# The L3 stage of a fused Perceiver kernel, written as one pipeline over tiles of four batches with a fixed TensorE order

## The chip, the cores and the metric

The kernel runs on one core of a Trainium2 chip. The metric is the device time of one execution in microseconds (us); of the kernel before there are three timed runs, and one more execution was taken by the hardware profiler. The engines are TensorE (PE; its weight loads are PEld), VectorE (DVE), ScalarE (ACT), GpSimd (POOL) and SyncE (SP, which issues most DMAs). Each engine takes the instructions of its own queue in order; between engines they wait on semaphores.

## The reference, cut to what matters

Four layers act on x of shape (128 batches, 32 tokens, 128 channels). Each layer has a cross part (xattn), an attention part (attn) and a feed-forward part (ffn). The change touches layer 3 alone:

- xattn: `x = x + rmsnorm(layernorm(x)) @ W_in + b_in + depool`, where the depooled context (Dg, 128x512 per group) was computed long before and lies in DRAM;
- attn: layernorm, one projection to q, k, v, then for each batch and each of 16 heads a 32x32 softmax attention with a relative position bias, the output projection, and `x = x + result + b_out`;
- ffn: layernorm, `relu(xn @ sign(W1) + b1) @ sign(W2) + b2`, added to x. W1 and W2 are reduced to -1, 0, 1 once, ahead of the loop.

All of it is float32. No token of one batch meets a token of another, so the 128 batches can be worked on in any grouping.

## The kernel before, in words

The 4096 rows of x are held in on-chip memory as eight **groups** X[0] to X[7] (128 partitions x 4 x 128; 16 batches each). A group has four **tiles** of four batches (128 rows). `L3` (L1783) runs nine rounds. Round `it` interleaves two generators with `abreast`, 12 pieces of the first against 6 of the second: the first is `xattn13` of group `it` followed by `L3_attn` of group `it`, the second is `L3_ffn` of group `it - 1`. A `yield` ends a piece.

**xattn13** (L1150) loads Dg by a DMA (L1153), takes two sets of statistics (DVE bn_stats and bn_aggr at L200 and L201, `ve` at L216, the power on POOL at L218, twice, with `v` and `s` on DVE at L206, L207, L210 between), normalises on DVE (`xn`, L224), transposes on PE (`pxt`, L231), copies on ACT (`xT`, L1159), multiplies (`ph`, L1163), prepares Dg on POOL (L1164, L1165), adds it to X on POOL (L1166) and adds `ph` to X on DVE (L237).

**L3_attn** (L1810) first does the group's front: statistics, `nb` on DVE (L1801), `xn` on ACT (L1804, four instructions), X plus `bo` on POOL (L1816), transposes (`pxt`, L231), `xT` on ACT (L1820), then `pq` (L1824) with `QT` (L1825), `pk` (L1828) with four masked copies `KM` (L1830), and `pv` (L1835) with `V` (L1836). Then, for each of its four tiles: scores `S` in four blocks of four matmuls (L1844), each block followed by the bias add `E` on DVE (L1845); the row maximum `m` on DVE (L1847); the subtraction on POOL (`E`, L1848); the exponential on ACT (L1849); `Vb`, the values spread into blocks, on POOL (L690); a yield; the 32x32 transposes `ET` on DVE (L1854); sixteen matmuls into `po` (L1859); reciprocal `nm` (L1861) and product `O` (L1863) on DVE; four transposes into `pot` (L1866), copied by ACT to `OT` (L1868); the projection `pw` (L1871), added to X on DVE (L1872); a yield.

**L3_ffn** (L1894) is: statistics, `nb`, `xn` on ACT, X plus `b2` on POOL (L1898), `pxt`, `xT` on ACT (L1902), four matmuls `ph` of 512 columns (L1907) with a relu on ACT each (`hT`, L1908), sixteen matmuls `po` (L1914), the addition to X (L237), and the DMA of the finished group to DRAM (L1918).

What sets the order: nothing in L3 is ordered by hand in the kernel before. A scheduler walks the traced instructions and puts them into the five queues by their dependences, their place in the trace and its own idea of their cost. `queue` (L482), which the kernel already uses in other stages, adds a dependence without a semaphore between successive instructions of one engine, so that their order in the queue is the traced order. On PE that is a fixed order; DVE, ACT and POOL stay with the scheduler.

Buffers around the change: `ht` holds two of each tile buffer (E, Vb, ET, O, OT, m, nm, and QT, KM, V of a group); `hs` and `hf` hold one of each; the PSUM pools hold two banks each: `hpm` (tag m: pxt, ph, pq, pk, pv), `hps` (tag s: the score blocks), `hpo` (tag o: po, pot, pw), `hpf` (tag f: the ffn).

Of the kernel before, what the change touches and what calls it, by code (L numbers as in the profile page):

```python
# [9 lines left out]
FP = mybir.dt.float32  # L10
I32 = mybir.dt.int32
U32 = mybir.dt.uint32
AF = mybir.ActivationFunctionType
ALU = mybir.AluOpType
AX = mybir.AxisListType
# [3 lines left out]
B, T, C = 128, 32, 128  # L19
NG = 8  # L20
NT = 32
H = 16
HD = 8
# [134 lines left out]
def abreast(gens):  # L158

    done = [0] * len(gens)  # L160
    live = set(range(len(gens)))
    while live:
        k = min(live, key=lambda k: (done[k] + 1) / gens[k][0])
        done[k] += 1
        if next(gens[k][1], None) is None:
            live.discard(k)


class Kern:
# [202 lines left out]
    def L0_xattn(self, W):  # L372
        nc = self.nc
        with self.pool("xw") as xw:
# [62 lines left out]
            with self.pool("xc") as xc, self.pool("xs", 2) as xs, \  # L437
# [5 lines left out]
                for n in range(B + 2):  # L443
                    g, i, b = n // 16, n // 4 % 4, n % 4
                    for m in (range(3) if n == 0 else (n + 2,)):
                        if m < B:
                            self.L0_xattn_load(tiles.setdefault(m // 4, {"cT": {}, "cN": {}, "E": {}, "T": {}, "QP": []}), m, xc)
                    t = tiles[n // 4] if n < B else None
# [82 lines left out]
    def L0_xattn_scores(self, st, t, b, js, xs, pss):  # L531

        nc, nsn = self.nc, t["nsn"]
        if js[0] == 0:
            if b == 0:
                t["TL"] = xs.tile([128, 2, 4, 4], FP, tag="TL", name="TL")
            t["E"][b] = xs.tile([128, 4, LK + 1], FP, tag="E", name="E", bufs=3)
            t["nm"] = xs.tile([128, 4], FP, tag="nm", name="nm")
            t["sm"] = xs.tile([128, 4], FP, tag="sm", name="sm")
        E, nm, sm = t["E"][b], t["nm"], t["sm"]  # L540
        for j in js:
            S = pss.tile([128, LK], FP, tag="s")
            for cb in range(2):
                self.follow(st, nc.tensor.matmul(S, lhsT=t["QP"][j][:, cb, b, :, :], rhs=t["cT"][b][:, cb, :], start=cb == 0, stop=cb == 1))  # L544
            m = nm[:, j:j + 1]
            nc.vector.tensor_reduce(m, S, AX.X, ALU.max, negate=True)  # L546
            nc.vector.tensor_tensor(m, m, nsn[:, b, j:j + 1], ALU.min)  # L547
            nc.scalar.activation(E[:, j, 0:LK], S, AF.Exp, bias=m, accum_out=sm[:, j:j + 1])  # L548
        if js[1] == 3:
            d = xs.tile([128, 4], FP, tag="d")  # L550
            nc.vector.tensor_tensor(d, nm, nsn[:, b, :], ALU.subtract)
            nc.scalar.activation(E[:, :, LK], d, AF.Exp)
            nc.vector.tensor_tensor(sm, sm, E[:, :, LK], ALU.add)
            nc.vector.reciprocal(sm, sm)  # L554
# [222 lines left out]
    def dispatch(self, pool, psum, tag, I8, n, k, E, NB):  # L777
# [10 lines left out]
        nc.vector.tensor_reduce(M[:, :, 1:n + 1], OH.rearrange("p i j e -> p e i j"), AX.X, ALU.add)  # L788
        S = pool.tile([128, E, n + 1], FP, tag="dS")
        on = pool.tile([128, E, n + 1], FP, tag="don")  # L790
# [5 lines left out]
        f = lambda x: x.rearrange("p e i -> p (e i)")  # L796
        nc.vector.tensor_tensor_scan(f(S), f(on), f(N1), 0.0, ALU.mult, ALU.add)
        yield 1
# [559 lines left out]
    def L2_xattn_tile(self, g, i, xT, KT, w, yc, ypq):  # L1358
# [15 lines left out]
        sm = yc.tile([128, 4, 4], FP, tag="sm")  # L1374
        return {"cT": cT, "cN": cN, "sm": sm, "E": {}, "ET": {}}

    def L2_xattn_scores(self, st, t, b, q, js, yc, yx, yps):
        nc = self.nc
        N = LK + T
        if q is not None:  # L1380
# [3 lines left out]
            t["E"][b] = yx.tile([128, 4, N], FP, tag="E", name="E")  # L1384
            t["ET"][b] = []
        nm, E, sm = t["nm"], t["E"][b], t["sm"]
# [394 lines left out]


    def L3(self, W):  # L1783
        nc = self.nc
        with self.pool("hq") as hq, self.pool("hs") as hs, self.pool("ht", 2) as ht, self.pool("hf") as hf, \
                self.pool("hpm", 2, PSUM) as hpm, self.pool("hps", 2, PSUM) as hps, self.pool("hpo", 2, PSUM) as hpo, \
                self.pool("hpf", 2, PSUM) as hpf:
            q = self.L3_ffn_signs(W["L3_ffn"], hq, hpf)
            for it in range(NG + 1):
                gens = []  # L1790
                if it < NG:
                    gens.append((12, chain(self.xattn13(it, W["L3_xattn"], hs, hpm), self.L3_attn(it, W["L3_attn"], hs, ht, hpm, hps, hpo))))
                if it:
                    gens.append((6, self.L3_ffn(it - 1, W["L3_ffn"], q, hf, hpf)))
                abreast(gens)

    def normed_act(self, pool, src, mv, rs, tag):

# [8 lines left out]

    def L3_attn(self, g, w, ls, lt, lpm, lps, lpo):  # L1810
        nc = self.nc
        rel = w["rel"].rearrange("p (h k) -> p h k", h=H)
        wo4 = w["wo"].rearrange("p (j c) -> p j c", j=4)
        mv, rs = self.stats(ls, self.X[g], 4, 1e-5)
        xn = self.normed_act(ls, self.X[g], mv, rs, "xn3")
        nc.gpsimd.tensor_tensor(self.X[g], self.X[g], w["bo"].unsqueeze(1).to_broadcast([128, 4, 128]), ALU.add)  # L1816
        ps = lpm.tile([128, 512], FP, tag="m", name="pxt")
        self.transposed(ps, xn)
        xT = ls.tile([128, 512], FP, tag="xT3")
        nc.scalar.copy(xT, ps)  # L1820
        yield 1
        QT = lt.tile([128, 16, T], FP, tag="QT")
        ps = lpm.tile([128, 16, T], FP, tag="m", name="pq")
        nc.tensor.matmul(ps, lhsT=w["wqkv"][:, 0:128], rhs=xT, start=True, stop=True)  # L1824
        nc.scalar.activation(QT, ps, AF.Copy, scale=HD ** -0.5)  # L1825
        KM = lt.tile([128, 4, 16, T], FP, tag="KM")
        ps = lpm.tile([128, 16, T], FP, tag="m", name="pk")
        nc.tensor.matmul(ps, lhsT=w["wqkv"][:, 128:256], rhs=xT, start=True, stop=True)  # L1828
        for k in range(4):
            nc.scalar.activation(KM[:, k], ps, AF.Copy, scale=self.hq[:, k:k + 1])  # L1830
        V = lt.tile([128, 4, H, HD + 1], FP, tag="V")
        nc.gpsimd.memset(V[:, :, :, HD:HD + 1], 1.0)
        ps = lpm.tile([128, 4, H, HD], FP, tag="m", name="pv")
        for i in range(4):
            nc.tensor.matmul(ps[:, i], lhsT=xT[:, i * 128:(i + 1) * 128], rhs=w["wqkv"][:, 256:384], start=True, stop=True)  # L1835
        nc.scalar.copy(V[:, :, :, 0:HD], ps)  # L1836
        yield 1
        for i in range(4):
            E = lt.tile([128, H, T], FP, tag="E")
            for j in range(4):  # L1840
                r = slice(32 * j, 32 * j + 32)
                S = lps.tile([128, 4, T], FP, tag="s")
                for b in range(4):
                    nc.tensor.matmul(S[32 * b:32 * b + 32], lhsT=QT[r, 4 * i + b, :], rhs=KM[r, :, 4 * i + b, :], start=True, stop=True)  # L1844
                nc.vector.tensor_tensor(E[:, 4 * j:4 * j + 4, :], S, rel[:, 4 * j:4 * j + 4, :], ALU.add)  # L1845
            m = lt.tile([128, H], FP, tag="m")
            nc.vector.tensor_reduce(m, E, AX.X, ALU.max)  # L1847
            nc.gpsimd.tensor_tensor(E, E, m.unsqueeze(2).to_broadcast([128, H, T]), ALU.subtract)  # L1848
            nc.scalar.activation(E, E, AF.Exp)  # L1849
            Vb = lt.tile([128, H, 4, HD + 1], FP, tag="Vb")  # L1850
            self.blocked(nc.gpsimd, Vb, V[:, i], HD + 1)
            yield 1
            ET = lt.tile([128, H, T], FP, tag="ET")
            nc.vector.transpose(ET.rearrange("p h t -> p (h t)"), E.rearrange("p h t -> p (h t)"))  # L1854
            ps = lpo.tile([128, 4, 4, HD + 1], FP, tag="o", name="po")
            for k in range(4):
                for j in range(4):
                    h = 4 * j + k
                    nc.tensor.matmul(ps[32 * j:32 * j + 32, k], lhsT=ET[:, h, :], rhs=Vb[:, h], start=True, stop=True)  # L1859
            nm = lt.tile([128, 4, 4], FP, tag="nm")  # L1860
            nc.vector.reciprocal(nm, ps[:, :, :, HD])  # L1861
            O = lt.tile([128, 4, 4, HD], FP, tag="O")
            nc.vector.tensor_tensor(O.rearrange("p b k d -> p k b d"), ps[:, :, :, 0:HD], nm.unsqueeze(3).to_broadcast([128, 4, 4, HD]), ALU.mult)  # L1863
            pt = lpo.tile([32, 4, 4, T], FP, tag="o", name="pot")
            for b in range(4):
                nc.tensor.transpose(pt[:, b].rearrange("p j q -> p (j q)"), O[:, b].rearrange("p k d -> p (k d)"), self.ident)  # L1866
            OT = lt.tile([32, 4, 4, T], FP, tag="OT")
            nc.scalar.copy(OT, pt.rearrange("p b j q -> p j b q"))  # L1868
            pw = lpo.tile([128, 128], FP, tag="o", name="pw")
            for j in range(4):  # L1870
                nc.tensor.matmul(pw, lhsT=OT[:, j].rearrange("p b q -> p (b q)"), rhs=wo4[:, j, :], start=j == 0, stop=j == 3)  # L1871
            nc.vector.tensor_tensor(self.X[g][:, i, :], self.X[g][:, i, :], pw, ALU.add)  # L1872
            yield 1


    def L3_ffn_signs(self, w, qw, qpb):
# [58 lines left out]
```

## Time and profile before

| What | us |
|---|---|
| median of three runs | 5003.25 |
| lowest, highest of them | 4987.8, 5008.44 |
| the profiled execution, its own time | 5049.65 |
| its span, first to last instruction | 5047.9 |
| first statistics of L3's group 0 | at 4688.8 |
| first scores of group 0 (S, L1844) | at 4711.5 |
| starts of `pq` (L1824), groups 0 to 7 | 4705.2, 4739.9, 4784.7, 4826.5, 4875.5, 4915.1, 4955.6, 4992.3 |
| last addition of `pw` to X (L1872) | at 5029.0 |
| last addition of the ffn to X (L237) | at 5044.0 |

Times in the profile are counted from the span's start. A page gives each engine's busy time, the span in 40 slices with the granted TensorE clock (PEclk; 1.00 is full speed), the chain of work that ended last, and the costliest groups of instructions by line; the trace can be asked for the same in any window, for who waited for whom, and for the instructions in order of time. A PE count is of records: one float32 matmul of this kernel is two records, a transpose one.

### The profile page before, as it was taken

The page shows a single profiled execution, that of the slowest core. Times are in us where ns is not written, and L with a number is a line of the kernel's source. Part 1 is how long each engine was busy: PE and PEld are TensorE (multiplying, and loading weights), DVE is VectorE, ACT ScalarE, POOL GpSimd, SP SyncE. Part 2 cuts the span into 40 slices and gives each one's busy share as a digit, 9 for nine tenths or more (in the row PEclk, how much of TensorE's full clock was granted, in tenths as well). Part 3 has the DMA queues.
Part 4 walks back from the last instruction along what each step waited for, and adds up shares of the span by engine and source line. Part 5 has one row for each costly group of instructions (what it writes and reads, how often), then busy time and mean ns, then how long its engine had stood idle before and what let it go on. Part 6 is the DMA issues. An engine that isn't in the chain of part 4 may idle for free. (4 is left out here: it accounts for less than half of the span.)

```text
span 5047.9 us, 90278 instructions
## 1 busy us (share of the span) xinstructions
PE 4255.4 (84%) x33802; PEld 3110.6 (62%) x33802; DVE 3389.1 (67%) x10311; ACT 2350.5 (47%) x6637; POOL 1292.9 (26%) x1309
## 2 busy tenths in 40 slices
PE   7999999999898989875367788988898886879688
PEld 5777676767676766665255565666566653446455
DVE  5336758494948585776645378988898775877444
ACT  4555445454454444422134344545554553763333
POOL 1020211111111102135043522332332323322443
PEclk8999898999999999957588898999999997999677
DMA  4223131314141312245133410010101110000100
GB/s 138 60 59 58 42 63 47 61 42 68 38 73 33 59 49 56 64 99 145 32 99 88 136 44 24 26 33 25 29 28 33 37 42 19 1 1 16 37 12 11
DMA packets 388969, 255.96 MB, mean 51 GB/s; under 512 B 184545, under 2 KB 356961, under 8 KB 388017
## 3 DMA queue, kind: packets, MB, share of 16 engines
q1 hardware_dynamic: 361842, 191.22, 16.2%
q0 software_dynamic: 18240, 58.66, 4.1%
q8 instruction: 267, 4.37, 0.4%
q10 hardware_dynamic: 8448, 0.30, 0.2%
q14 instruction: 172, 1.41, 0.1%
HBM read 211.02 MB, written 39.08 MB: 50 GB/s over the span
## 5 line engine op out<-in xcount | busy, mean ns | idle before, releaser
L218 POOL TENSOR_TENSOR rs<-ve,w_const 128x4 f32<-128x4 f32 (+1 forms) x192 | 190.2, 991 | 1567.4 <-DVE ve L216 1285.8
L544 PE MATMUL S<-cT,q 128*128 128x257 f32 x2048 | 545.2, 406 | 19.3 <-ACT E L548 18.5
L544 PEld LDWEIGHTS S<-cT,q 128*128 128x128 f32 x2048 | 389.7, 200 | 146.9 <-issue 53.9
L546 DVE TENSOR_REDUCE nm<-S 128x1 f32<-128x257 f32 x512 | 214.2, 419 | 337.9 <-PE S L544 336.8
L1389 PE MATMUL S<-cT,QM 128*128 128x289 f32 x1024 | 325.0, 434 | 76.3 <-ACT E L1391 69.7
L548 ACT ACTIVATE E<-S,nm 128x257 f32<-128x257 f32 x512 | 242.7, 475 | 297.5 <-DVE nm L547 296.5
L1391 ACT ACTIVATE E<-S,nm 128x289 f32<-128x289 f32 x512 | 253.7, 500 | 188.8 <-DVE nm L1390 184.7
L724 DVE TENSOR_TENSOR A<-A,elt 128x400 f32<-128x400 f32 (+22 forms) x608 | 290.7, 478 | 4.2
L722 DVE TENSOR_TENSOR elt<-A,row 128x400 f32<-128x400 f32 (+22 forms) x608 | 288.5, 474 | 6.4
L527 PE MATMUL pq<-xT,WQK 128*128 128x128 f32 x2048 | 270.9, 292 | 13.4 <-ACT q L528 13.4
L1389 PEld LDWEIGHTS S<-cT,QM 128*128 128x128 f32 x1024 | 177.0, 197 | 159.0 <-ACT E L1391 69.4
L583 PE MATMUL po<-TA,cN 128*128 128x512 f32 x512 | 270.0, 610 | 4.7 <-DVE xn L224 3.9
L527 PEld LDWEIGHTS pq<-xT,WQK 128*128 128x128 f32 x2048 | 255.5, 202 | 23.7 <-ACT q L528 16.7
L584 PE MATMUL po<-TB,cN 128*128 128x512 f32 x512 | 265.6, 600 | 0.0
L558 ACT ACTIVATE E<-E,sm 128x256 f32<-128x256 f32 x512 | 220.2, 498 | 79.4 <-DVE sm L554 74.5
L241 POOL TENSOR_TENSOR QM<-QT,w_const 128x512 f32<-128x512 f32 x128 | 140.8, 1105 | 438.4 <-PE S L1389 412.9
L1390 DVE TENSOR_REDUCE nm<-S 128x1 f32<-128x289 f32 x512 | 219.9, 449 | 30.0 <-PE S L1389 27.0
L1400 PE MATMUL pt<-w_const,E 128*96 128x128 f32 (+1 forms) x1536 | 235.7, 290 | 0.0
L597 PE MATMUL pout<-WVO,OT 128*128 128x128 f32 x2048 | 234.2, 275 | 0.3 <-ACT OT L585 0.3
L597 PEld LDWEIGHTS pout<-WVO,OT 128*128 128x128 f32 x2048 | 231.7, 192 | 0.9 <-ACT OT L585 0.5
L1400 PEld LDWEIGHTS pt<-w_const,E 128*96 128x96 f32 (+1 forms) x1536 | 182.7, 146 | 61.7 <-issue 37.4
L1721 ACT ACTIVATE E<-S,nm 128x128 f32<-128x128 f32 x512 | 180.3, 399 | 64.5 <-DVE nm L1718 64.5
(526 smaller groups left out, 10351.1 us busy)
## 6 DMA issues: line engine op xcount, KB each, us to landing
cT<-ctxT SPq DMA_DIRECT2D x128, 257.0 KB
cN<-ctx SPq DMA_DIRECT2D x128, 256.0 KB
cT<-ctxT SPq DMA_DIRECT2D x32, 514.0 KB
phik<-PW SPq DMA_DIRECT2D x32, 256.0 KB
phiq<-P SPq DMA_DIRECT2D x32, 256.0 KB
A<-phik SPq DMA_DIRECT2D x128, 64.0 KB
PQ<-phiq SPq DMA_DIRECT2D x32, 256.0 KB
cN<-ctx SPq DMA_DIRECT2D x32, 194.0 KB
```

Source lines behind the costliest of these rows:

```text
L527: self.follow(st, nc.tensor.matmul(ps[:, k, :, :], lhsT=WQK[:, 4 * j + k, cb * 128:(cb + 1) * 128], rhs=t["x"], start=True, stop=True))
L544: self.follow(st, nc.tensor.matmul(S, lhsT=t["QP"][j][:, cb, b, :, :], rhs=t["cT"][b][:, cb, :], start=cb == 0, stop=cb == 1))
L548: nc.scalar.activation(E[:, j, 0:LK], S, AF.Exp, bias=m, accum_out=sm[:, j:j + 1])
L558: nc.scalar.activation(E[:, j, 0:256], E[:, j, 0:256], AF.Copy, scale=sm[:, j:j + 1])
L583: self.follow(st, nc.tensor.matmul(po, lhsT=cN[:, 0, c], rhs=TA, start=True, stop=False), nc.tensor.matmul(po, lhsT=cN[:, 1, c], rhs=TB, s ...
L584: nc.tensor.matmul(po, lhsT=cN[:, 1, c], rhs=TB, start=False, stop=True))
L597: self.follow(st, nc.tensor.matmul(po[:, 0, :], lhsT=OT[:, cb, h, :, :], rhs=WVO[:, cb, h, :], start=h == 0 and cb == 0, stop=False))
L722: nc.vector.tensor_tensor(t, A[:, k, :, i0:i1].rearrange("p h i -> p i h").unsqueeze(3).to_broadcast([128, m, HC, n]), row[:, :, i0:N].uns ...
L724: nc.vector.tensor_tensor(A[:, i0:i1, :, i0:N], A[:, i0:i1, :, i0:N], t, ALU.subtract)
L1389: self.follow(st, nc.tensor.matmul(S, lhsT=t["QM"][:, 0, 4 * j:4 * j + 4, :], rhs=t["cT"][:, b, :], start=True, stop=True))
L1391: nc.scalar.activation(E[:, j, :], S, AF.Exp, bias=nm[:, j:j + 1], accum_out=sm[:, j, b:b + 1])
L1400: self.follow(st, nc.tensor.transpose(pt[0:n, j * 128:(j + 1) * 128], E[:, j, k0:k1], self.ident))
```

## The change

L3 becomes a loop over n = 0 to 33 that works on three tiles at once. `L3_attn` is cut into five parts with the same instructions: `L3_attn_front` (everything up to V), `L3_attn_scores` (S to Vb), `L3_attn_values` (ET, po, nm, O), `L3_attn_turn` (pot, OT) and `L3_attn_end` (pw, the addition to X). Step n traces, in this order: the turn of tile n-2, the scores of tile n, a piece of the next group's prologue, the values of tile n-1, a piece of ffn, the end of tile n-2, a piece of prologue, a piece of ffn. After each, `order` chains the newly traced PE instructions with `queue`, so PE's order is exactly the traced one.

The prologue of group g+1 (xattn13, then the front) is started at the first step of group g; it has four pieces, so it is traced in the first and second step of the group: first step `pxt` and `ph` of xattn, second step `pxt` of the front and `pq`, `pk`, `pv`. The ffn of a group is queued when its last tile has ended, which is in the second step of the next group; its five pieces then come as: `pxt` at the end of that second step, four `ph` in the third step, sixteen `po` in the fourth. No instruction is added or removed, no buffer count is changed.

```diff
     def L3(self, W):
...
-            for it in range(NG + 1):
-                gens = []
-                if it < NG:
-                    gens.append((12, chain(self.xattn13(it, W["L3_xattn"], hs, hpm), self.L3_attn(it, W["L3_attn"], hs, ht, hpm, hps, hpo))))
-                if it:
-                    gens.append((6, self.L3_ffn(it - 1, W["L3_ffn"], q, hf, hpf)))
-                abreast(gens)
+            w = W["L3_attn"]
+            st, traced = {}, nc.cur_bb.bb.instructions
+            at = len(traced)
+            def order():
+                nonlocal at
+                self.queue(st, *[i for i in traced[at:] if i.engine == nc.tensor.engine])
+                at = len(traced)
+            grp = {}
+            def pro(g):
+                return chain(self.xattn13(g, W["L3_xattn"], hs, hpm), self.L3_attn_front(g, w, hs, ht, hpm, grp)) if g < NG else iter(())
+            new, ffn, fq, units = pro(0), iter(()), [], {}
+            for _ in new:
+                order()
+            def side(k):
+                nonlocal ffn
+                if k == 0:
+                    next(new, None)
+                else:
+                    if next(ffn, None) is None and fq:
+                        ffn = self.L3_ffn(fq.pop(0), W["L3_ffn"], q, hf, hpf)
+                        next(ffn, None)
+                order()
+            for n in range(NT + 2):
+                g, i = n // 4, n % 4
+                if i == 0 and n < NT:
+                    for _ in new:
+                        order()
+                    new = pro(g + 1)
+                if n > 1:
+                    pt = self.L3_attn_turn(units[n - 2], ht, hpo)
+                if n < NT:
+                    units[n] = self.L3_attn_scores(grp[g], i, w, ht, hps)
+                order()
+                side(0)
+                if 0 < n <= NT:
+                    self.L3_attn_values(units[n - 1], ht, hpo)
+                order()
+                side(1)
+                if n > 1:
+                    self.L3_attn_end((n - 2) // 4, (n - 2) % 4, units.pop(n - 2), w, hpo)
+                    if n % 4 == 1:
+                        fq.append(n // 4 - 1)
+                order()
+                side(0)
+                side(1)
+            for _ in ffn:
+                order()
+            while fq:
+                for _ in self.L3_ffn(fq.pop(0), W["L3_ffn"], q, hf, hpf):
+                    order()
```

## The prediction

> **What bounds the kernel now.** I read the page first, to see where L3 lies and how TensorE does there.
>
> ```profile
> span 5047.9 us, 90278 instructions
> ...
> PE   7999999999898989875367788988898886879688
> ...
> PEclk8999898999999999957588898999999997999677
> ```
>
> L3 is the last three slices (about 360 us, 7% of the span): PE looks busy, but its granted clock is 0.6 to 0.7 where most other stages have 0.9. Then the busy times of the stage in one window, and who PE and VectorE waited for in it:
>
> ```profile
> core 0: us, PE busy (x) PEld busy (x) DVE busy (x) ACT busy (x) POOL busy (x), PEclk, DMA share, GB/s
> 4690.00:5028.00 338.00, 277.83 (x2961) 177.13 (x2962) 161.01 (x586) 121.29 (x224) 147.89 (x138) 0.72 0.05 14
> ```
>
> ```profile
> PE po L1859 <- DVE ET L1854: 18.6, 13, 5.5
> PE pxt L231 <- ACT xn L1804: 10.5, 6, 5.2
> PE pxt L231 <- DVE xn L224: 8.8, 1, 8.8
> PE po L1859 <- DVE mv L201: 6.5, 4, 1.7
> ```
>
> No engine is full: PE is busy 82% at a clock of 0.72, VectorE and POOL under half. L3 is bound by a chain that runs through all engines, and PE is slow because it pauses. The instructions in order of time show the chain, once per group:
>
> ```profile
> 4906.64 0.69 DVE L237 TENSOR_TENSOR X<-X,ph 128x512 f32<-128x512 f32 x1
> ...
> 4909.83 1.02 POOL L218 TENSOR_TENSOR rs<-ve,w_const 128x4 f32<-128x4 f32 x1 [3.12 <-DVE ve L216]
> ...
> 4911.12 1.64 ACT L1804 ACTIVATE xn<-X,nb,rs 128x128 f32<-128x128 f32 x4
> ...
> 4915.06 2.07 PE L1824 MATMUL pq<-xT,w_L_attn 128*128 128x512 f32 x2 [0.68 <-ACT xT L1820]
> ...
> 4922.35 0.18 PEld L1844 LDWEIGHTS S<-KM,QT 32*32 32x32 f32 x16 [0.76 <-ACT KM L1830]
> ```
>
> From the addition of `ph` to the next group's first scores it is 15.7 us. `pq` starts 40 us apart: 4705.2 to 4992.3 is seven groups in 287.1, **41.0 us per group** (34.7 to 49.0). From first scores (4711.5) to the last addition of `pw` (5029.2) it is 317.7.
>
> **What the change does not alter.** No instruction comes or goes. Queues up to L3 are the same, with the same first group's front, so I keep 4711.5 for the first scores. The last ffn, alone after the last `pw`, stays serial (5029.2 to 5047.9). SP's queue differs in one place: a Dg load now stands ahead of the first output, and no compute waits for an output.
>
> **What it moves.** I read the queues of the changed program as built. In steady state PE does, per group, four steps: A: pot, S, pxt of xattn, po, pw, ph; B: pot, S, pxt of the front, po, pw, pq, pk, pv, pxt of the ffn; C: pot, S, po, two ffn ph, pw, two ph; D: pot, S, po, eight ffn po, pw, eight po. VectorE has the tile's ET ahead of the next tile's score additions, and in A to B: ET, then X plus ph, then the additions of B. POOL has a Vb ahead of the E of A, C and D, and in B: E, rs (front), X plus bo, rs, Vb, rs (both for the next xattn), X plus Dg, rs (ffn), Dg twice, X plus b2. PE can no longer slip other matmuls into a gap, so whatever is late on those queues holds everything behind it.
>
> **The floor, if nothing waited.** PE at full clock, from rows of the timeline (distance to the next instruction): pot and pxt 0.44, po 0.40, pw 1.08, xattn ph 1.1, eight ffn po 1.96, one ffn ph or pq or pk 0.86, pv 1.0; S about 1.4, because its third block waits for the first block's addition (two PSUM banks). Four tiles are 4 x 3.32 = 13.3; the rest is 3 x 0.44 + 1.1 + 1.7 + 1.0 + 3.4 + 3.9 = 12.4. Together 25.7 against 41.0 now. This is what the change could bring at best: 7 x 15.3 = 107 us.
>
> **One steady group, walked through.** Time 0 is the last scores of step A. Durations are the means of the groups by line in L3.
>
> To the front's transposes in B: pxt and po 0.9; Vb (POOL waits for po, because two buffers) 1.18, to 2.1; E 1.05, to 3.15; exponential 0.63, to 3.8; ET 0.71, to 4.55; X plus ph 0.69, to 5.25 (`ph` itself was done at 3.2: it is VectorE's order that holds it). Then VectorE has two additions 0.49, two bn_stats 0.4, two additions 0.5, two bn_aggr 0.25, m 0.69: 7.6; POOL's E 1.05, to 8.7; rs 1.02, to 9.75; nb 0.16; four xn 1.65, to 11.65; transposes done at **11.9**. PE had nothing allowed since B's scores (about 6.3): a gap of over 4 us.
>
> To the ffn's transposes at the end of B, all through POOL: X plus bo 1.27 (it must wait for the four xn), to 12.95; rs 1.0, to 14.0; Vb 1.18, to 15.2; rs 1.0, to 16.25; VectorE: s, four xn, and between them X plus pw, bn_stats, bn_aggr, 1.85, to 18.1; X plus Dg 1.28, to 19.4; rs 1.0, to 20.4; nb 0.2; four xn 1.65, to 22.3; transposes done at **22.55**. Beside this PE does po, pw, pq, pk, pv by about 18, half of it at half clock, which costs nothing there: the cover is 4.5 us. PE pauses again for 2.6 to 4.
>
> PE sets the rest. C: pot, S, po 2.5 (pot cold, 1.03 by its row), to 25.0; two ph at half clock 3.4 (the last ffn took 1.7 each when cold), to 28.4; pw 1.08; two ph 1.75, to 31.2 (E and exponential of C, held to 28.8 by Dg, X plus b2 and Vb on POOL, just do not delay the relus). D: 0.44 + 1.4 + 0.4 + 1.96 + 1.08 + 1.96 = 7.2, to 38.4. A again: 0.44 + 1.4: **40.2**. I counted some 19 hand-overs between engines at about 0.05 us; the timeline shows 0.03 to 0.14, so I add 0.04 each: **41.0 us per group**. The stalls of the four tiles go, but the two layernorm chains, which ran partly beside PE work, now stand in line in step B.
>
> The unknown is the clock after the two gaps, which the trace of before shows only for its own gaps. Lower end: full clock in C, 1.7 less for the two ph and 0.4 for pot, so 38.9 with the hand-overs. Upper end: half clock through C, D and A: pw 0.85 more twice, the other two ph 1.7, sixteen po 3.9, pots 0.85: 8.2 more, 49.2. I take the middle value, half clock until about 28, since the nearest rows show recovery after some 3 to 9 us:
>
> ```profile
> 4888.00:4891.00 3.00, 0.77 (x33) 0.61 (x35) 1.08 (x3) 1.21 (x2) 1.20 (x2) 1.00 0.00 0
> 4891.00:4894.00 3.00, 3.00 (x46) 2.51 (x32) 1.34 (x4) 0.00 (x0) 2.22 (x2) 0.58 0.02 5
> 4894.00:4897.00 3.00, 3.00 (x62) 2.21 (x60) 1.56 (x5) 1.11 (x2) 0.00 (x0) 0.85 0.00 0
> ```
>
> One pause of 2.2 us, and the clock (third number from the end) falls to half and is back some 4 us later. After 4909 it stayed at half until about 4918.4, with PE busy most of that time. The Trainium skill ("TensorE: Matmul & The Clock Gate", Part 1) says that the clock halves after about one idle window of 3.4 us and is full again after one busy window as long; its table at the end asks for no gap above about 3 us, which speaks against a fixed order with a gap of over 4. By that rule alone the second cold stretch costs 1.7 instead of 2.1 per group, 2 us over all groups; the rows here show a shorter pause sufficing and a longer recovery.
>
> **The sum.** First scores to last `pw` addition: first tile 1.4; group 0, which has no ffn and no earlier tiles but the same first chain, 30; six steady groups 6 x 41.0 = 246; the last group and the drain 31.6 (step A 5, the ffn's transposes at 11, C 8.7, D 7.2, to 27; then pot, po and pw of the last two tiles, one after another with nm, O and OT between, 4.6). Together 309 against 317.7: **9 us less**. On the profiled execution that is 5049.65 - 9 = 5040.6; that execution was 46 us over the median of the three runs, and I apply the difference to the median: 5003.25 - 9, **about 4994 us**. Differences under 0.5% (25 us) are about what a measurement of this kernel cannot tell from no change.
>
> **Rivals.** (1) PE-bound steps: the statistics come early enough that B hardly waits. For it: VectorE and POOL are under half busy, and the statistics of the next xattn do move a whole group ahead. Against it: nothing of the front's chain can start before X plus ph. With both chains at half their length beyond PE's own work the group is about 31: 6 x 10 less than forecast, and a little in group 0: 4930. (2) Slower: PE's clock stays at half after the gaps of B, through C, D and A; 49.2 per group, 6 x 8.2 and 6 more in the last group: 5049. It decides from about 5 of those 8.2 us (46 to 47 per group) on. For it: the stage has 0.72 now, and from 4813 to 4828 the clock was at half although PE was busy 2.2 to 3.0 of every 3 us. Against: from 4960 to 4981 it was full with PE as dense as in my C and D. (3) The fixed order costs at every tile: in S, VectorE is busy with ET or a Vb-delayed chain when the third block needs its bank, and nothing may be slipped in; 0.4 us more for 32 tiles is 13 us: 5007.
>
> **Chances and range.** Forecast (38.5 to 43.5 per group, so 15 us either way): 0.66, of which 0.11 lies below the 0.5% bound and 0.02 above it. Rival 1: 0.09, rival 2: 0.17, rival 3: 0.08. Faster 0.11 + 0.09 = 0.20, same 0.53 + 0.08 = 0.61, slower 0.02 + 0.17 = 0.19. Rival 2 comes in degrees, from its point of decision (25 us over the median, 5028) to 5049. The range is the forecast's 15 us with the spread of the runs (about 10) added, and reaches up to 5038, the middle of rival 2: **4965 to 5038**. Outside it lie rival 1, half of rival 2 and some tails, 0.09 + 0.085 + 0.02, just under 2 in 10.
>
> **What would show it.** Right: in step B the front's `pxt` waits for xn on ACT by 4 to 5 us and the ffn's `pxt` by 2 to 5, once per group each; X plus ph starts right behind an ET and not behind `ph`; `pq` starts 39 to 43 us apart; waits of po for ET are gone; the clock falls to half twice per group. Wrong: `pq` under 36 apart (the chains overlap more than the queues say) or over 45 with the clock at 0.5 through the ffn's matmuls; or a wait in S or po that I have at nothing.

## The result, and the profile after

The changed kernel takes 5018.40 us (median of 20 runs, 4999.49 to 5030.58) against 5001.74 of the kernel before in the same session (20 runs, 4987.8 to 5011.76): ratio 1.0032, 95% interval 1.0023 to 1.0041. It is **slower by 16.7 us**; 9 us less had been forecast.

Between two profiled executions the stages ahead of L3, which are the same, differ by tens of us (first scores at 4711.5 before, at 4667.4 after), so I compare L3 from its first scores to its last addition of `pw`, here the one window of that length in the changed kernel (busy us and records of PE, PEld, DVE, ACT, POOL; then the clock):

```profile
4667.40:5000.59 333.19, 256.96 (x2936) 164.07 (x2936) 157.28 (x550) 116.50 (x213) 135.91 (x128) 0.73 0.04 12
```

That is 333.2 us against 317.7 (4711.5 to 5029.3): 15.5 more, close to the 16.7 by which the medians differ. `pq` starts 42.2, 44.8, 44.5, 44.4 and 44.4 us apart from the third on (41.0 on average before). The mean clock is the 0.73 of before. The waits of PE in the stage (us in total, times, longest):

```profile
PE pxt L231 <- ACT xn L1849: 47.8, 14, 4.5
PE S L1891 <- DVE E L1892: 25.5, 32, 7.0
PE pw L1928 <- ACT OT L1921: 1.3, 3, 0.7
```

The waits of `po` for ET are gone, as foretold. In their place PE waits for the xn of the two layernorms, fourteen times, and once 7.0 us in S. One steady group on PE, in order of time (start, duration; a wait in brackets):

```profile
4840.51 0.45 PE L1891 MATMUL S<-KM,QT 32*32 32x128 f32 x16
4842.51 0.62 PE L1891 MATMUL S<-KM,QT 32*32 32x128 f32 x16 [1.55 <-DVE E L1892]
4847.36 1.63 PE L231 MATMUL pxt<-w_const,xn 128*128 128x128 f32 x4 [4.24 <-ACT xn L1849]
...
4858.42 1.61 PE L231 MATMUL pxt<-w_const,xn 128*128 128x128 f32 x4 [2.48 <-ACT xn L1849]
...
4863.30 3.78 PE L1963 MATMUL ph<-xT,q_w 128*128 128x512 f32 x4
4867.01 2.07 PE L1928 MATMUL pw<-w_L_attn,OT 32*128 32x128 f32 x8
4869.02 3.29 PE L1963 MATMUL ph<-xT,q_w 128*128 128x512 f32 x4
4872.15 0.60 PE L1919 MATMUL pot<-w_const,O 128*32 128x128 f32 x4
```

The step's scores are held 1.55 us by VectorE; then come the two pauses that the prediction walked through, the front's transposes and the ffn's. What follows the second, step C up to the end of its last `ph` at 4872.3, takes 12.3 us: each pair of `ph` 3.3 to 3.8, `pw` 2.07, about twice their time at full clock (1.98 and 1.15 in other groups). The clock (third number from the end) in windows of 1 us says why:

```profile
4843.00:4844.00 1.00, 0.12 (x6) 0.00 (x0) 1.00 (x6) 0.00 (x0) 0.00 (x0) 1.00 0.00 0
4844.00:4845.00 1.00, 0.00 (x0) 0.00 (x0) 0.97 (x6) 0.00 (x0) 0.58 (x1) 0.69 0.00 0
...
4854.00:4855.00 1.00, 1.00 (x4) 0.41 (x3) 1.00 (x7) 0.27 (x1) 0.00 (x0) 0.69 0.00 0
...
4857.00:4858.00 1.00, 0.00 (x0) 0.00 (x0) 0.16 (x1) 1.00 (x3) 0.57 (x1) 1.00 0.09 28
4858.00:4859.00 1.00, 0.58 (x2) 0.36 (x2) 0.00 (x0) 1.00 (x3) 0.00 (x0) 0.51 0.77 230
...
4866.00:4867.00 1.00, 1.00 (x2) 0.00 (x0) 0.35 (x1) 0.62 (x2) 0.00 (x0) 0.50 0.00 0
...
4871.00:4872.00 1.00, 1.00 (x3) 0.32 (x2) 0.00 (x0) 0.69 (x1) 0.00 (x0) 0.66 0.00 0
```

It falls at 4844.4 (0.69 in that window is 0.38 us at 1.0 and the rest at 0.5), is back at 4854.6, falls again at 4858.0, and is back only at 4871.7, although PE was busy all through 4862 to 4871.

### The profile page after: what moved, and what is told of

Same layout as the page of the kernel before. It is cut to its first block, busy times and chain, and to the rows that moved or that the text cites. A ratio compares the mean times of both kernels' runs of the same rounds, so it can differ in the third digit from the quotient of the medians.

```text
span 5020.2 us, 90277 instructions
## 1 busy us (share of the span) xinstructions
PE 4232.2 (84%) x33802; PEld 3100.5 (62%) x33802; DVE 3397.6 (68%) x10311; ACT 2349.7 (47%) x6637; POOL 1293.8 (26%) x1309
## 5 line engine op out<-in xcount | busy, mean ns | idle before, releaser
L527 PEld LDWEIGHTS pq<-xT,WQK 128*128 128x128 f32 x2048 | 255.0, 202 | 23.5 <-ACT q L528 16.6
```

The source lines that it names most:

```text
L527: self.follow(st, nc.tensor.matmul(ps[:, k, :, :], lhsT=WQK[:, 4 * j + k, cb * 128:(cb + 1) * 128], rhs=t["x"], start=True, stop=True))
```

## The experiments

**Theories.** Clock theory: the second pause, ahead of the ffn's transposes, halves the clock through the whole of step C, where PE is on the path, and this is most of the 24 us between forecast (309) and measurement (333). Rival: the waits in step B themselves, or the fixed order at each tile, cost more than reckoned, and the clock is a bystander. Apart from this stands the question of why the change does not win at all; there the theory is that the fixed order on PE keeps it from doing anything in the pauses, while the traced order of the steps is a gain.

Each ratio is to the kernel before on the same chip in the same session, with its 95% interval; the L3 length is from one profiled execution. The chips differ: the kernel before has 5000.9 to 5050.5 us on them.

| Run | ratio to before | L3, us | steady `pq` distance |
|---|---|---|---|
| before | 1 | 317.7 | 34.7 to 49.0 |
| changed kernel | 1.0032 [1.0023, 1.0041] | 333.2 | 44.4 |
| changed, second chip | 1.0032 [1.0018, 1.0046] | 332.9 | 44.4 |
| fillers 4 and 2 | 1.0018 [1.0007, 1.0029] | 328.6 | 44.5 |
| fillers 0 and 2 | 0.9993 [0.9978, 1.0009] | 311.9 | 41.0 |
| fillers 4 and 5 | 0.9976 [0.9964, 0.9988] | 317.0 | 40.7 |
| two buffers for Dg | 1.0033 [1.0022, 1.0045] | 333.6 | 44.4 |
| Dg behind E of C | 1.0031 [1.0020, 1.0042] | 325.5 | 44.4 |
| fillers 0 and 2, Dg behind E | 0.9978 [0.9965, 0.9992] | 306.7 | 39.4 to 41.1 |
| PE free | 0.9923 [0.9905, 0.9942] | 277.3 | 35.4 to 36.9 |
| fixed, spread, late | 0.9958 [0.9945, 0.9971] | 292.3 | 37.8 |
| the same with fillers 3 and 0 | 0.9950 [0.9930, 0.9969] | 292.5 | 37.7 |
| PE free, spread, late | 0.9915 [0.9897, 0.9933] | 273.0 | 34.2 |
| the same, Dg behind E | 0.9914 [0.9901, 0.9928] | 274.5 | 34.1 |

### Fillers in the two pauses

PE is given 128x512 matmuls whose result the transposes overwrite, ahead of the transposes of each layernorm; all else is as in the changed kernel. They do no useful work: they are there to keep PE busy. The first number of `warm` is for the front's transposes, the second for the ffn's; the last ffn, which runs alone, gets none.

```diff
+            self.warm = (4, 2)
...
+            self.warm = (0, 0)
             for _ in ffn:
...
         ps = lpm.tile([128, 512], FP, tag="m", name="pxt")
+        for _ in range(self.warm[0]):
+            nc.tensor.matmul(ps, lhsT=self.ident, rhs=self.sel, start=True, stop=True)
         self.transposed(ps, xn)
...
         ps = qpf.tile([128, 512], FP, tag="f", name="pxt")
+        for _ in range(self.warm[1]):
+            nc.tensor.matmul(ps, lhsT=self.ident, rhs=self.sel, start=True, stop=True)
         self.transposed(ps, xn)
```

With four and two, expected:

> The changed kernel with work that computes nothing on PE ahead of the transposes that wait: four 128x512 matmuls before the front's pxt and two before the ffn's pxt, written into the same PSUM tile and overwritten by the transposes; not before the last ffn, which runs alone. The queues of the other engines stay as they were but for a few instructions of the first group. Theory (the clock): PE's granted clock falls to half in the second pause of step B and stays there through step C, which took 12.3 us instead of 8.7; kept busy, PE is at full clock in C, the group falls from 44.4 to about 41 us, and the whole to about 4998 us (20 less than the changed kernel, a little under the kernel before). Rival (the pauses themselves and the order are the cost, the clock a symptom): 5015 to 5021, groups stay at 44.

Measured: L3 328.6, `pq` still 44.5 apart. PE in a late group:

```profile
4884.84 1.13 PE L1871 MATMUL pq<-xT,w_L_attn 128*128 128x512 f32 x2
...
4887.65 1.88 PE L1961 MATMUL pxt<-w_const 128*128 128x512 f32 x4
4892.92 1.63 PE L231 MATMUL pxt<-w_const,xn 128*128 128x128 f32 x4 [3.39 <-ACT xn L1851]
...
4897.81 3.78 PE L1969 MATMUL ph<-xT,q_w 128*128 128x512 f32 x4
```

The first pause was filled, so `pq` ran at full clock (1.13 us against 2.08; the two records are one matmul) and PE was done sooner; but the ffn's xn came no sooner, so behind the two fillers (the row with w_const alone) there were still 3.39 us of nothing, the clock fell, and `ph` took 3.78. The miss was in the experiment: it lengthened the pause that it should have filled. With fillers in the second pause alone:

> As the run before, with only the two matmuls before the ffn's pxt; every queue but PE's is that of the changed kernel. Theory, narrow form (the second pause alone puts step C at half clock): the same 20 us less, about 4998. Theory, wide form (the clock's fall after the first pause also counts, the second only prolongs it): less than half of that, 5008 to 5015. Rival (the clock is a symptom): 5015 to 5021.

```profile
4885.01 1.88 PE L1961 MATMUL pxt<-w_const 128*128 128x512 f32 x4
4887.66 1.47 PE L231 MATMUL pxt<-w_const,xn 128*128 128x128 f32 x4 [0.77 <-ACT xn L1851]
...
4891.52 3.35 PE L1969 MATMUL ph<-xT,q_w 128*128 128x512 f32 x4
4894.80 1.15 PE L1932 MATMUL pw<-w_L_attn,OT 32*128 32x128 f32 x8
4895.89 1.98 PE L1969 MATMUL ph<-xT,q_w 128*128 128x512 f32 x4
```

Two matmuls without use made the stage 21.3 us shorter (333.2 to 311.9). The ratio, 0.9993, goes with it: this is the narrow form of the theory. The pause left is 0.77 us; the clock still falls, but only from 4890.9 to 4894.3, over the first pair of `ph` (3.35), and is back for `pw` and the second pair (1.15, 1.98). Those are the durations that the prediction had put into step C, and the period is the 41.0 that it had worked out. Both pauses filled, with enough in the second:

> Four 128x512 matmuls without use ahead of the front's transposes and five ahead of the ffn's, so that PE has work through both pauses. In the earlier run with four and two, the filled first pause let pq, pk and pv go at full clock, so the ffn's transposes came due 3.4 us after the two fillers, and the clock fell there. Theory (it is the length of the second pause, after whatever PE last did, that halves the clock in step C): the wait before the ffn's transposes goes below 1 us, the clock stays at 1.0 through C, and pq is 38.5 to 41 us apart, L3 295 to 308 us, 0.3 to 0.6% faster than the kernel before. Rival (fillers in the first pause cost as much as they give, by holding up what follows on PE): pq 43 to 45 apart, L3 320 to 330, whatever fills the second.

`pq` 40.7 apart: the clock in the first pause is worth 0.3 us per group, since what follows there is covered by the chain through POOL, as the prediction had it. L3 is 317.0 in its profile, not 295 to 308: one group took 43.6, and group 0 2 us longer than with fillers in the second pause alone. The ratio, 0.9976, gives 12 us less than before where this profile gives 1; I cannot say which of the two is typical of that kernel. The rival, that fillers in the first pause cost what they give, is out at 40.7.

### The changed kernel on a second chip

> The changed kernel itself once more, unaltered, so that the edits have it beside them on one chip. Theory: pq 44 to 45 us apart in the steady groups, L3 (first scores to the last addition of pw) 332 to 335 us, and 0.2 to 0.4% slower than the kernel before. Rival (the result belongs to one chip): within 0.1% of the kernel before, with L3 still 333.

1.0032, L3 332.9, 44.4 apart: the result does not hang on the chip.

### The 7.0 us wait in group 0

In group 0 PE waits 6.98 us at the scores of the third tile. POOL of the changed kernel at that time:

```profile
4686.28 1.28 POOL L1166 TENSOR_TENSOR X<-X,Dg 128x512 f32<-128x512 f32 x1 [1.32 <-DVE xn L224]
4690.70 1.09 POOL L1164 TENSOR_TENSOR Dg<-Dg,w_L_xattn 128x512 f32<-128x512 f32 x1 [3.15 <-DMA Dg<-dd]
4691.87 1.26 POOL L1165 TENSOR_TENSOR Dg<-Dg,w_L_xattn 128x512 f32<-128x512 f32 x1
4693.09 1.17 POOL L690 TENSOR_TENSOR Vb<-V,w_const 128x576 f32<-128x576 f32 x1
4694.23 1.05 POOL L1895 TENSOR_TENSOR E<-E,m 128x512 f32<-128x512 f32 x1
```

X plus Dg frees the one Dg buffer, the next load starts, and POOL, whose next instruction needs it, stands 3.15 us with Vb and E behind it; ET and the next additions wait for that E. The first trial gave Dg a second buffer:

```diff
-        Dg = hs.tile([128, 4, 128], FP, tag="Dg")
+        Dg = hs.tile([128, 4, 128], FP, tag="Dg1" if g % 2 and getattr(self, "two", 0) else "Dg", name="Dg")
...
+            self.two = 1
```

> The changed kernel with two buffers for Dg instead of one, so that a group's Dg is loaded a group ahead. In group 0 of the changed kernel PE waits 7.0 us at the scores of the third tile: POOL stands 3.15 us at Dg, whose load only starts when X plus Dg has read the one buffer, with Vb and E of that tile queued behind it. Theory: that wait falls to 3.5 to 4.5 us, POOL's waits for Dg go, group 0 (the second pq to the third) falls from 38.9 to 34 to 36.5, and the steady groups stay at 44 to 45 because C's half clock covers POOL there; L3 328 to 331. Rival 1 (Dg is also on the path of the steady groups): pq under 43 apart, L3 under 322. Rival 2 (another wait is right behind): no change in any group.

Nothing moved (39.3 us between the second and third `pq`, L3 333.6), rival 2's case. POOL still waits there:

```profile
4720.13 1.28 POOL L1166 TENSOR_TENSOR X<-X,Dg 128x512 f32<-128x512 f32 x1 [1.32 <-DVE xn L224]
4724.80 1.09 POOL L1164 TENSOR_TENSOR Dg<-Dg,w_L_xattn 128x512 f32<-128x512 f32 x1 [3.39 <-DMA Dg<-dd]
```

The scheduler, given a buffer more, put the Dg of one group further ahead into the same place of POOL's queue: it is the fifth Dg there and not the fourth. Its load is issued at 4721.43, right behind the same X plus Dg, whose buffer it takes over. So the place in the queue had to change, not the buffer. The second trial orders it behind the E of step C:

```diff
         nc.gpsimd.tensor_tensor(Dg, Dg, w["ginit"].unsqueeze(1).to_broadcast([128, 4, 128]), ALU.mult)
+        if g > 2 and hasattr(self, "subs"):
+            self.queue({}, self.subs[4 * (g - 3) + 2], nc.cur_bb.bb.instructions[-1])
...
         nc.gpsimd.tensor_tensor(E, E, m.unsqueeze(2).to_broadcast([128, H, T]), ALU.subtract)
+        self.subs.append(nc.cur_bb.bb.instructions[-1])
```

`subs` lists the subtractions E of the tiles in their order.

> The changed kernel with the first multiplication of Dg held behind the E of step C in POOL's queue (its load still has one buffer). Two buffers alone had moved nothing, because POOL's queue then takes up the Dg of the group after, at the same place, and waits for its load just as long. Theory (in group 0 it is the place of Dg in POOL's queue, ahead of Vb and E of the third tile, that makes PE wait 7.0 us at its scores): that wait falls to 1 to 3 us, group 0 (second pq to third) from 39 to 31 to 35 us, the clock falls less there; the steady groups stay at 43.5 to 44.5, as C's half-clock matmuls cover POOL; L3 324 to 329 us. Rival (the wait there comes from elsewhere, po or the exponential): group 0 stays at 38 to 39, L3 332 to 334. Rival 2 (Dg is on the steady groups' path too): pq under 43 apart, L3 under 320.

```profile
4740.39 1.27 POOL L1168 TENSOR_TENSOR X<-X,Dg 128x512 f32<-128x512 f32 x1 [1.32 <-DVE xn L224]
4741.85 1.18 POOL L690 TENSOR_TENSOR Vb<-V,w_const 128x576 f32<-128x576 f32 x1 [0.19 <-PE po L1913]
4742.98 1.05 POOL L1898 TENSOR_TENSOR E<-E,m 128x512 f32<-128x512 f32 x1
...
4745.27 1.09 POOL L1164 TENSOR_TENSOR Dg<-Dg,w_L_xattn 128x512 f32<-128x512 f32 x1 [1.09 <-DMA Dg<-dd]
```

The wait in S fell from 7.0 to 1.65 us, the distance from the second `pq` to the third from 39.1 to 34.1, L3 to 325.5, and the steady groups stayed at 44.4: the theory's numbers. The median does not show these 7.7 us (1.0031 against 1.0032 and 1.0033, each uncertain by 0.0011 to 0.0014, which is some 6 us); this step rests on the traces.

### Both repairs

> The changed kernel with both repairs: two matmuls without use ahead of the ffn's transposes, and Dg held behind the E of step C on POOL. Alone the first took L3 from 333 to 312 us and the second to 325.5. Theory (they are two separate causes, and nothing else is missing from the forecast): they add, 333 - 21 - 7.5 = L3 302 to 307 us, group 0 33 to 35, steady groups 40.5 to 41.5, 0.2 to 0.3% faster than the kernel before. Rival (a shorter group 0 or Dg's new place lengthens the second pause, so that two fillers no longer hold the clock): steady groups 43 to 44.5, L3 318 to 326, 0 to 0.2% slower.

L3 306.7, group 0 33.7, steady groups 39.4 to 41.1, ratio 0.9978 [0.9965, 0.9992]: 11 us less than before. The two add but for 2.5 us (333.2 - 21.3 - 7.7 would be 304.2), and the stage ends 2.3 us below the 309 that was forecast. Part of that closeness is luck: by the table below, the six groups are 3.5 us shorter than forecast and the end 1.3 us longer.

### PE left free

The traced order of the steps stays; only the chaining of PE's instructions is dropped, so that the scheduler places them.

```diff
             def order():
                 nonlocal at
-                self.queue(st, *[i for i in traced[at:] if i.engine == nc.tensor.engine])
                 at = len(traced)
```

> The same traced order without the fixed order on PE: the scheduler is free on PE as on the other engines. Theory A (what costs is that PE may slip nothing into a pause): back to the kernel before or better, 4985 to 5003. Theory B (what costs is the traced order, with the prologue's four pieces in two steps and the ffn's start right behind the last tile): 5012 to 5022.

0.9923, L3 277.3: 40 us less than before and 56 less than with the fixed order. PE around the front's transposes:

```profile
4915.30 0.63 PE L1890 MATMUL S<-KM,QT 32*32 32x128 f32 x2 [0.46 <-DVE E L1891]
4915.86 0.47 PE L231 MATMUL pxt<-w_const,xn 128*128 128x128 f32 x1
4916.27 0.65 PE L1890 MATMUL S<-KM,QT 32*32 32x128 f32 x8
4916.85 0.47 PE L231 MATMUL pxt<-w_const,xn 128*128 128x128 f32 x1
4917.25 0.64 PE L1890 MATMUL S<-KM,QT 32*32 32x128 f32 x6
```

Where the fixed order makes PE wait 4.24 us for all of xn, here the scores of the next tile lie between the transposes, each of which goes as soon as its quarter of xn is there. So of the change's two parts the step order, with PE left to the scheduler, is worth 40 us, and the fixed order on top of it costs 56; the difference is the 15.5 us lost.

### The pieces spread, the ffn a step later

The fixed order kept, one prologue piece per step instead of two, and the ffn's first piece one step later, so that the front's transposes move to step C and `pq`, `pk`, `pv` to step D.

```diff
-                    if n % 4 == 1:
+                    if n > 4 and n % 4 == 2 or n == NT + 1:
                         fq.append(n // 4 - 1)
                 order()
-                side(0)
                 side(1)
```

> The fixed order kept, with the two chains that wait given a step of lead: one piece of the prologue per step instead of two (xattn pxt in A, ph in B, the front's pxt in C, pq, pk, pv in D), and the ffn queued one step later (its pxt at the end of C, ph in D, po in the next A). If the pauses of step B are what costs, by themselves and through the clock: groups of 31 to 36 us, 4940 to 4975. If VectorE's and POOL's queues just hold PE at other places: groups of 40 or more, 4995 to 5025.

0.9958, L3 292.3, `pq` about 38 apart: a gain, but not down to the 31 to 36 expected. With three fillers ahead of the front's transposes (as above, 3 and 0):

> The fixed order kept, one prologue piece per step, the ffn a step later, and three 128x512 matmuls without use ahead of the front's transposes, where PE pauses 3.4 us in the version without them (L3 292.3, pq 37.7 apart, the clock at half from there through pq, pk and pv). Theory (here too the half clock after the pause is on the path, since pw, pot, S and pq stand behind it with little else to wait for): the clock stays at 1.0, pq 33.5 to 35.5 apart, L3 268 to 282, 0.7 to 1.0% faster than the kernel before. Rival (VectorE's and POOL's chain to the ffn's transposes sets that step, at any clock): pq 36.5 to 38, L3 285 to 295.

Nothing more was won (292.5, 37.7), the rival's case. The fillers held the clock at 1.0 until 4896.8, 6.4 us after the step's scores and not just 3.0 us, but then it fell all the same. PE around it:

```profile
4890.40 2.84 PE L1863 MATMUL pxt<-w_const 128*128 128x512 f32 x6
4893.84 0.71 PE L231 MATMUL pxt<-w_const,xn 128*128 128x128 f32 x2 [0.60 <-ACT xn L1850]
...
4900.00 1.01 PE L1922 MATMUL pot<-w_const,O 128*32 128x128 f32 x4 [1.29 <-DVE O L1916]
...
4903.47 0.91 PE L1894 MATMUL S<-KM,QT 32*32 32x128 f32 x16 [1.86 <-DVE E L1895]
```

`pot` waits for O and S for the additions, both on VectorE behind the ffn's and the xattn's statistics: these are the waits that end last here, though that the chain through VectorE sets the step is read from the rows and not tried by a run. How much of the clock is left in that step stays open, since the fillers did not hold it at 1.0.

### Free, spread and late together, and the best version

> No fixed order on PE, and of the other work one prologue piece per step with the ffn queued a step later: the two edits that each gained, together. Theory A (with PE free the pauses are filled anyway, so spreading the pieces adds little): pq 34 to 36 us apart, L3 268 to 282, 0.7 to 1.0% faster than the kernel before. Theory B (spreading also takes the two layernorm chains apart on VectorE and POOL, which PE's freedom doesn't): pq 29 to 33 apart, L3 235 to 262, 1.1 to 1.6% faster.

L3 273.0, 34.2 apart, 0.9915 [0.9897, 0.9933]: theory A. A free PE already has most of what spreading gives. With Dg behind E of step C as well:

> No fixed order on PE, one prologue piece per step, the ffn a step later, and Dg held behind E of step C on POOL. Beside the 272.9 us of the version without the last edit. Theory: group 0 falls from 32 to 28 to 31, the steady groups stay at 34 to 34.5 (they are held by the front's chain in the step after A and the half clock that follows), L3 266 to 272, about 0.9% faster than the kernel before. Rival: Dg now stands in the way of the next tile's Vb: steady groups 35 to 36, L3 275 to 285.

274.5 and 0.9914 [0.9901, 0.9928]: neither theory's gain nor the rival's loss. These two and the version with PE merely free cannot be told apart by their intervals; all three beat both kernels, the kernel before by 0.8 to 0.9%, some 40 us.

## Why the prediction was wrong

The forecast of 309 us for the stage had three terms; measured in the changed kernel, up to the last scores of step A of groups 1 and 7 (4703.2 and 4965.8):

| Term | forecast | changed kernel | both repairs |
|---|---|---|---|
| first tile and group 0 | 31.4 | 35.8 | 31.3 |
| six groups | 246 | 262.6 | 242.5 |
| last group and drain | 31.6 | 34.8 | 32.9 |
| sum | 309 | 333.2 | 306.7 |

- **The step that failed: "I take the middle value, half clock until about 28, since the nearest rows show recovery after some 3 to 9 us."** Relative to the same zero (4837.0) it lasted until 34.7. Step C took 12.3 us and not 8.65, so the term of 246 for the six groups was too small by 16.6; with the fillers step C had the predicted durations, and the period was 41.0. The rows of before that I leaned on stood after other pauses: 2.2 us, back after 4, and one back after 9. The mechanism was seen, and rival 2 named it; but rival 2 let the clock stay low through C, D and A and got 49.2, and the forecast took it off after the first `ph` pair; the truth, all of C and no more, lies between, at 44.4, below the point of 46 to 47 from which I let rival 2 decide.
- **Group 0, "30", was too small by 4.4.** It had no walk of its own. The walk of the steady group had "X plus Dg, rs (ffn), Dg twice" and priced Dg's two instructions, not the landing of its load, which only starts when X plus Dg has ended. In the steady groups POOL waits 2.03 us there too, but their period stayed at 44.4 when Dg was moved, so it is covered there. In group 0 nothing covers it.
- **The last group and the drain, 31.6, were too small by 3.2.** With the two fillers alone this term is 32.9, so 1.9 of it went with the clock; the other 1.3 stays open.
- **Right: both chains of step B.** Front's transposes done at 4849.0, 12.0 after zero (predicted 11.9); the ffn's at 4860.0, 23.0 (22.55); pauses of 4.24 and 2.48 us (4 to 5, 2 to 5); X plus `ph` at 4841.60 right behind the ET of 4840.96; D 7.3 us (7.2); waits of `po` for ET gone. That half clock beside the first chain costs nothing held as well: 40.7 with it filled, 41.0 without. (The row of 10.5 us that the prediction shows for these waits in the kernel before takes in the last ffn; up to 5028 it is 7.6 us in five waits. No term of the sum rests on it.)
- **Rival 1**, PE-bound steps, needed the chains to overlap with PE's work. With the fixed order they do not; with PE free they overlap more, and the group takes 35.5. **Rival 3**, a wait in S at every tile, is not there: 0.39 us, as reckoned in the 1.4, except in step B (1.55) and group 0.
- The sign turned because the forecast's 9 us was a small difference between a gain and a cost that were each far larger (40 and 56), and the price of one cold stretch, 3.6 us per group, is 21 us over the stage. The 0.5% that the prediction took for the least that a measurement can tell was too much: with 20 runs of each kernel the interval is 1.0023 to 1.0041.

The Trainium skill ("TensorE: Matmul & The Clock Gate", Part 1) lets the clock be full again after one busy window of 3.4 us. Here the clock fell at 4858.0 and was back 13.7 us later, although PE was busy through the whole of 4864.9 to 4868.3, and by that rule the forecast would have come out 2 us lower still. Its table at the end asks for no gap above some 3 us, and the pause of 2.48 us here was shorter and still cost the clock. The measurement decides. The same section says that the window runs freely, and that agrees: see below.

## What to carry to other kernels

A fixed order on an engine turns every late operand into a pause of that engine: before fixing it, walk the dependence chain that ends at each instruction and ask what could run meanwhile; with a good traced order, leaving the engine to the scheduler may keep the gain without the pauses. Price a pause by what runs at half clock after it, not by its own length: here 2.5 us of waiting cost 3.6 us more behind it, and two matmuls without use bought that back. Where a single-buffered load is consumed on an in-order queue, the wait for its landing belongs to everything behind it in that queue, and a second buffer does not help if the consumer just moves ahead with it.

## What the runs showed of the hardware

- The changes of the granted clock lie on a grid. From the 1 us windows: down at 4844.4, up at 4854.6, down at 4858.0, up at 4871.7, so 10.2, 3.4 and 13.7 us apart, or 3, 1 and 4 times 3.4. With the fillers it was down from 4890.9 to 4894.3 (3.4), and with both pauses filled from 4929.9 to 4933.3 (3.4). The grid does not start with a pause: the first pause began at 4843.1 and the clock fell 1.3 us later, the second at 4855.9 and it fell 2.1 us later.
- How many stretches of the grid it stays down differs. In the steady groups PE was busy without a gap for two whole stretches before the clock came back (4847.8 to 4854.6 and 4864.8 to 4871.7); after the filled second pause, in the runs with fillers 0 and 2 and 4 and 5, one was enough. The stretch ahead of the fall does not tell the two apart: in group 1 of the changed kernel PE was busy 1.38 of 3.4 us there (4724.9 to 4728.3), in the steady group 1.34 (4854.6 to 4858.0), and in group 1 one whole stretch was enough (4731.7 to 4735.1). What decides was not tried.
- The idle time of a stretch does not decide alone whether the clock falls. With fillers 0 and 2 the stretch ahead of the fall (4887.5 to 4890.9) holds only the last 0.2 us of the 0.77 us pause, and PE is busy 2.71 of its 3.4 us; with both pauses filled (4926.5 to 4929.9) it holds nothing of the 0.83 us pause, and PE is busy 2.84. Yet with both pauses filled a stretch with PE busy only 1.89 us (4827.5 to 4830.9) kept the clock at 1.0. In the first two PE did mostly transposes and 32x32 scores, in the third scores and fillers; whether the kind of work decides was not tried.
